# Convolution and attention layers on one Trainium2 core: the small maps written in two halves, the second tile's keys at a step's head, the first image's second chunk of values in a tile of its own

## The chip, the cores and the metric

One core of a Trainium2 chip runs the whole kernel as a single launch. The metric is device time in microseconds. The engines are named as the profile names them: PE multiplies matrices, DVE is the vector engine, ACT the scalar engine (it evaluates activations), POOL is GpSimd, and SP issues most of the DMA transfers. [...]

## The reference, cut to what matters

The input is 8 images of 256 channels and 64 x 64 pixels in float32. Two layers follow one another, each added to its input after a group normalisation.

```python
# layer 0: weights of a 3x3 window, made per pixel
x1, x2, x3 = conv1x1(x, w1, b1), conv1x1(x, w2, b2), conv1x1(x, w3, b3)   # 32, 32, 256 channels
h = relu(bn1(concat([x1, unfold3(reflect_pad(x2))])))                     # 320 channels
w = conv1x1(relu(bn2(conv1x1(h, cw1))), cw2, cb2)                         # 9 taps for 32 groups
out = einsum('bgskhw,bgkhw->bgshw', unfold3(zero_pad(x3)), w)
...
# layer 1: attention in a 7x7 window of each pixel, and a weighted depthwise branch
pe = einsum('dc,chw->dhw', Wp, position) + bp
q, k, v = conv1x1(x, Wq, bq) * 64 ** -0.5, conv1x1(x, Wk, bk), conv1x1(x, Wv, bv)   # 4 heads of 64
att = softmax(q . (unfold7(reflect_pad(k)) + unfold7(reflect_pad(pe))))
out_att = att . unfold7(reflect_pad(v))
wts = softmax over 9 of (Wfc x);  out_conv = sum over 9 of depthwise(relu(depthwise(x))) * wts
return rate1 * out_att + rate2 * out_conv
```

## The kernel before, in words

An image is cut into 8 bands of 8 rows (`NB`, `R`), 64 bands in all. The main loop runs over `g`, the band of layer 1; layer 0 runs 12 bands ahead of it (`AHEAD`), so that `g` begins at -12 and the last 12 bands have no layer 0 beside them. A band has 8 steps `s`: two halves of the channels (`ct`) times four pairs of 8 x 8 query tiles (`m`). I count steps from 0 and call them step 0 to step 7.

The order of the work is written out by hand. Within a step of layer 1 PE does, in even steps, the scores (L747, tile `sco`) and the weighted values (L796, into the PSUM bank `small`), and in every step two matrices of branch weights `pf` (L883) and the transposes of probabilities `ptp` (L784). ACT takes the exponentials of scores (L769) and of `pf` (L888), and scales the probabilities (L778). DVE masks the scores (L761), takes the reciprocal of their sum (L776) and does the taps of the depthwise branch (L840, L866).

`beside` puts the other work of a step into three lists. `head` is issued at the beginning of the step, before its exponentials; `mid` after the first `pf`; `end` behind everything. An entry may hand back a function that runs later, so that PE's part is issued first and the part of ACT or DVE behind it. `advance` divides a step into six places, and `after(n, f)` puts `f` off by n of them.

- `small_maps` (L324) makes, in step 0, two 1x1 convolutions of layer 0 for the band `g + 12` in the upper part of the bank `small`; PE's part is L332. `write_maps` (L339) copies them into the tile `x2` with eight activations on ACT (six at L347, two at L351): four for the upper four rows, four for the lower. Then POOL adds border columns and rows (L355, L356, L361, L362). `hidden_maps` (L411) reads `x2` for its relus (L422). The next use of `small` is L796 in step 2.
- `value_maps` makes the larger map of layer 0, in two parts: `p3` (L373) at the end of step 0 and in the middle of step 1, each copied to `x3n` by ACT (L378) and stored by SP (L380).
- `tap_weights` makes `pw` (L468) at the end of steps 1 to 5. DVE multiplies it with the map (L481, two products each) and POOL adds the products (L489).
- `queries` (L681, copied by ACT at L685) and `keys` (L703) are made once for each half of the channels. DVE finishes the keys with one large and three small operations (L711, L718). For the second half of the channels the keys stand in the middle of step 3, but in the first and last band of an image in step 2.
- `gn_affine` makes the coefficients of the group normalisations with small matmuls (L242) and DVE operations, in the fourth and the seventh band of an image, beginning in step 2.
- `values` (L598, copied by ACT at L605 into the tile `vc`) makes values for a band in two chunks. `store_values` stores them to DRAM with eight SP transfers (L618, L622), `mirror_rows` adds border rows there (L629), and `value_tile` loads them as `vt` (L640). For the first two bands of an image this is done during the last band of the image before, and for the first image in the band g = -1.
- `position` (L647) makes the position map `pe` on POOL (L655) for each of the first image's bands and stores it for the other images (L661, SP).

Most matmul results, `pf`, `ptp`, `p3`, `pw`, `pq`, `pk` and `pv`, share four PSUM buffers with the tag `gen`, which are handed out in turn: a tile waits for the readers of the fourth one before it. The bank `small` has one buffer, `vc` one, `ex` (SBUF, for the exponentials of `pf`) three.

Of the kernel before, what the change touches and what calls it, by code (L numbers as in the profile page):

```python
# [10 lines left out]
F32 = mybir.dt.float32  # L11
# [7 lines left out]
P = 128  # L19
C = 256  # L20
# [3 lines left out]
R = 8  # L24
BAND = R * W
NB = H // R
# [15 lines left out]
HR = R + 2  # L42
# [19 lines left out]
AHEAD = NB + 4  # L62
# [25 lines left out]
def conv_layers_kernel(ctx: ExitStack, tc: tile.TileContext, ins: dict, out: bass.AP):  # L88
    nc = tc.nc
# [130 lines left out]
    def after(n, f):  # L220
        later.append((place[0] + n, f))
# [102 lines left out]
    def small_maps(b, i, home):  # L324


        im = images[b]

        p12 = home[:, 2 * P :].rearrange("p (r c) -> p r c", r=R // 2)
        for kt in range(NCT):  # L330
            for u in range(2):
                nc.tensor.matmul(  # L332
                    p12[64 * u : 64 * u + 64], im.w12s[:, kt, :],
                    im.xc[i][:, kt, u * BAND // 2 : (u + 1) * BAND // 2],
                    start=(kt == 0), stop=(kt == NCT - 1),
                )
        return lambda: write_maps(b, i, p12)

    def write_maps(b, i, p12):  # L339
        im = images[b]  # L340
        t = im.x2[i] = w0.tile([P, HR, W], F32, tag="x2", name=f"x2_{b}_{i}", bufs=2)
        bias = im.bias
        for u in range(2):
            r, o = u * R // 2, 64 * u
            for q, (dst, src) in enumerate(((1, 0), (0, 0), (0, 1))):
                n = W - (q != 1)
                nc.scalar.activation(  # L347
                    t[32 * q : 32 * q + 32, r + 1 : r + 1 + R // 2, dst : dst + n],
                    p12[o : o + 32, :, src : src + n], AF.Identity, bias=bias[o : o + 32, 0:1],
                )  # L350
            nc.scalar.activation(  # L351
                t[96:128, r : r + R // 2, :], p12[o + 32 : o + 64], AF.Identity, bias=bias[o + 32 : o + 64, 0:1]
            )

        nc.gpsimd.tensor_copy(t[0:32, 1 : 1 + R, 0:1], t[0:32, 1 : 1 + R, 2:3])  # L355
        nc.gpsimd.tensor_copy(t[64:96, 1 : 1 + R, W - 1 : W], t[64:96, 1 : 1 + R, W - 3 : W - 2])  # L356

        if i == 0:
            nc.gpsimd.tensor_copy(t[0:96, 0, :], t[0:96, 2, :])
        else:  # L360
            nc.gpsimd.tensor_copy(t[0:96, 0, :], im.x2[i - 1][0:96, R, :])  # L361
            nc.gpsimd.tensor_copy(im.x2[i - 1][0:96, R + 1, :], t[0:96, 1, :])  # L362
        if i == NB - 1:
            nc.gpsimd.tensor_copy(t[0:96, R + 1, :], t[0:96, R - 1, :])
# [218 lines left out]
    def values(b, j, half):  # L583

        im = images[b]
        if half == 0:
            im.vc[j] = w1.tile([P, R // 2, C], F32, tag="vc", name=f"vc_{b}_{j}", bufs=1)
        vc, yp = im.vc[j], im.yp[min(j, NB - 1)]  # L590
        first, last, _ = value_rows(j)
        pv = ps.tile([P, 2, C], F32, tag="gen", name=f"pv_{b}_{j}_{half}", bufs=4)
        for g in range(2):
            r = first + 4 * half + 2 * g
            if r >= last:
                break
            for kt in range(NCT):
                nc.tensor.matmul(  # L598
                    pv[:, g], yp[:, kt, r : r + 2].rearrange("p r c -> p (r c)"), wv[:, kt],
                    start=(kt == 0), stop=(kt == NCT - 1),  # L600
                )
            n = g + 1

        def take():
            nc.scalar.copy(vc[:, 2 * half : 2 * half + n], pv[:, :n])  # L605

        return take
# [39 lines left out]
    def position(b, i):  # L647

        first, last = new_keys(i)
        n, a = last - first, i * R + first  # L650
        pe = images[b].pe[i] = w1.tile([P, KW - PAD, W], F32, tag="pe", name=f"pe_{b}_{i}", bufs=1)
        if b:
            nc.sync.dma_start(out=pe[:, :n], in_=kept[i])
            return
        nc.gpsimd.tensor_add(  # L655
            pe[:, :n],
            pecol.unsqueeze(1).to_broadcast([P, n, W]),
            perow[:, a : a + n].unsqueeze(2).to_broadcast([P, n, W]),
        )
        kept[i] = dram.tile([P, n, W], F32, tag=f"pe{i}", name=f"pe_{i}", bufs=1)  # L660
        nc.sync.dma_start(out=kept[i], in_=pe[:, :n])  # L661

    kept = {}

# [67 lines left out]
    half = [slice(0, HD), slice(HD, P)]  # L732
# [71 lines left out]
    def small_tile(nm):  # L804

        return ps.tile([P, 4 * P], F32, tag="small", name=f"small_{nm}")
# [117 lines left out]
    def beside(g, s):  # L924

        b, i = divmod(g, NB)
        bn, inx = divmod(g + 1, NB)
        head, mid, end = [], [], []

        early = i in (0, NB - 1)  # L930
        if g >= 0:
            if s == 2:
                mid.append(lambda: keys(b, i, 1) if early else queries(b, i, 1))
            if s == 3 and early:
                head.append(lambda: queries(b, i, 1))
            if s == 3 and not early:
                mid.append(lambda: keys(b, i, 1))
        edge = inx in (0, NB - 1)
        if 0 <= g + 1 < B * NB:
            if s == 5 - edge:  # L940
                mid.append(lambda: position(bn, inx))
            if s == 6:
                mid.append(lambda: keys(bn, inx, 0) if edge else queries(bn, inx, 0))
            if s == 7:
                head.append(lambda: queries(bn, inx, 0) if edge else keys(bn, inx, 0))

        made = [(b, i + 2, (4, 5))] if g >= 0 and i < NB - 1 else []
        if i == NB - 1 and 0 <= b + 1 < B:
            made = [(b + 1, 0, (3, 4)), (b + 1, 1, (5, 7))]
        for bb, j, d in made:  # L950
            if s in d and (j < NB or s == d[0]):
                mid.append(lambda bb=bb, j=j, d=d: values(bb, j, d.index(s)))
            if s == d[1]:
                end.append(lambda bb=bb, j=j: store_values(bb, j))
            if s == d[1] + 1 and j in (0, NB):
                end.append(lambda bb=bb, j=j: mirror_rows(bb, j))
            if s == 7 and j != 1:
                for u in range(NT // 2):
                    end.append(lambda bb=bb, j=j, u=u: value_tile(bb, j, u))
        if g >= 0 and i == 0 and s in (0, 2):  # L960
            for u in (s, s + 1):
                mid.append(lambda u=u: value_tile(b, 1, u))

        nxt = [(b, i + 2, 0)] if g >= 0 and i + 2 < NB else []
        if i == NB - 1 and 0 <= b + 1 < B:
            nxt = [(b + 1, 0, 0), (b + 1, 1, 2)]
        for bb, ii, d in nxt:
            if s == d:
                end.append(lambda bb=bb, ii=ii: load_rows(bb, ii))
            if s in (d + 1, d + 2):  # L970
                end.append(lambda bb=bb, ii=ii, d=d: normalise(bb, ii, s - d - 1))

        alone = g < 0
        if 0 <= g + AHEAD < B * NB:
            bq_, iq = divmod(g + AHEAD, NB)
            if alone and s == 0:
                mid.append(lambda: small_maps(bq_, iq, small_tile(f"{bq_}_{iq}"))())
            if s == (2 if alone else 0):
                (mid if alone else end).append(lambda: value_maps(bq_, iq, 0, alone))
            if s == (3 if alone else 1):  # L980
                mid.append(lambda: value_maps(bq_, iq, 1, alone))
        if 0 <= g + AHEAD - 1 < B * NB and s == (2 if alone else 1):
            bh, ih = divmod(g + AHEAD - 1, NB)

            def hidden():
                parts = hidden_maps(bh, ih, alone)
                if not alone:
                    convs.extend(parts)

            end.append(hidden)  # L990
        if 0 <= g + AHEAD - 2 < B * NB and s in TAPS_AT[g < -1]:
            u = TAPS_AT[g < -1].index(s)
            end.append(
                lambda: tap_weights(*divmod(g + AHEAD - 2, NB), u, g < -1, PRODUCTS_AT[g < -1][u])
            )
        return head, mid, end
# [24 lines left out]
    with tc.manual_schedule():  # L1021
# [17 lines left out]
        for n, f in enumerate(layer1_loads()):  # L1039
            after(4 * STEPS * (3 + n), f)  # L1040

        pending, before, conv, convs = [], None, None, []
        for g in range(-AHEAD, B * NB):
            b, i = divmod(g, NB)
            for s in range(STEPS):
                ct, m = divmod(s, NT // 2)
                head, mid, end = beside(g, s)
                steer(g, s)
                if g >= 0:
                    nm = f"{b}_{i}_{ct}_{m}"  # L1050
                    weighted = []
                    if m % 2 == 0:
# [3 lines left out]
                        small = small_tile(nm)  # L1056
                        weighted, pending = weigh_steps(pending, small), []
                        if s == 0 and g + AHEAD < B * NB:
                            mid.append(small_maps(*divmod(g + AHEAD, NB), small))
                        if s in (4, 6) and convs:  # L1060
                            convs.pop()(small)
                        if before is not None:
# [140 lines left out]
```

## Time and profile before

| | |
|---|---|
| median of 3 runs (lowest to highest) | 3902.41 us (3900.53 to 3902.47) |
| the profiled execution: its own time | 3901.4 us |
| its span, first to last instruction | 3899.5 us |
| mean granted clock of PE | 0.994 |
| first score matmul of the band g = 0 | 233.4 us |
| an ordinary band (2178.4 to 2236.0) | 57.6 us |

"Busy" is the time in which an engine had an instruction running. Ends of matmuls are modelled, so that the time between the starts of two matmuls is safer to read than the end of one. A line of the timeline has the start, the duration, the engine, the line in the kernel, the operation, the tile written and the tiles read, the size and the number of instructions in a row; in brackets stand the idle time before it and what ended it. A line of the waits has who waited for whom, the total in us, how often, and the longest.

### The profile page before, as it was taken

What the parts mean: (1) busy time and instruction counts of PE and PEld (TensorE: products, weight loads), DVE (VectorE), ACT (ScalarE), POOL (GpSimd) and SP (SyncE); (2) the same over time, 40 slices, a digit from 0 to 9 for tenths busy, and PEclk for the clock granted to TensorE, in tenths of its full rate; (3) what the DMA queues carried; (4) which work ended last, traced back from release to release, by engine and by line L of the source; (5) the groups of instructions that cost most, each with busy time, mean ns of one, the idle gap of its engine ahead of it and who ended that gap; (6) DMA issues with size and microseconds to landing.
All of it is one profiled execution on the core that took longest, in us unless ns stands there. A gap on an engine that the chain in (4) does not pass through costs nothing.

```text
span 3899.5 us, 71759 instructions
## 1 busy us (share of the span) xinstructions
PE 3774.0 (97%) x24620; PEld 2112.0 (54%) x24620; DVE 3415.8 (88%) x7125; ACT 2809.8 (72%) x6770; POOL 3118.1 (80%) x2100
## 2 busy tenths in 40 slices
PE   6889999999999999999999999999999999999998
PEld 3445555555555555555555555555555555555554
DVE  6879999889988989899998998989988889978777
ACT  4457777777777777777777777777777777677776
POOL 4768888888987988888888888978988888955665
PEclk9999999999999999999999999999999999999999
DMA  8754544544544543544544544454543543332221
GB/s 247 211 162 128 142 113 126 155 124 113 136 127 131 148 120 104 151 137 118 145 112 136 143 124 116 132 145 119 139 113 102 145 123 101 89 94 81 78 66 37
DMA packets 438926, 490.14 MB, mean 126 GB/s; under 512 B 62016, under 2 KB 324256, under 8 KB 438304
## 3 DMA queue, kind: packets, MB, share of 16 engines
q1 hardware_dynamic: 421984, 469.79, 43.4%
q10 hardware_dynamic: 16576, 15.76, 1.3%
q8 instruction: 194, 3.18, 0.3%
q14 instruction: 172, 1.41, 0.1%
HBM read 343.76 MB, written 145.10 MB: 125 GB/s over the span
## 4 chain that ended last, share of the span: by engine, by line
PE 38%; POOL 22%; DVE 20%; ACT 10%; issue 5%; DMA 4%; SPq 0%; ACTq 0%; POOLq 0%; DVEq 0%
PE pf L883 18%; POOL xg L489 10%; POOL ex L1099 7%; DVE prod L481 6%; DVE rec L904 4%; DVE acc L866 4%; PE small L796 3%; ACT x L347 3%; PE pv L598 3%; PE ptp L784 3%; PE sco L747 3%; PE pq L681 2%; PE pk L703 2%; DMA x<-x3n 2%; ACT ex L888 2%
## 5 line engine op out<-in xcount | busy, mean ns | idle before, releaser
L883 PE MATMUL pf<-yp,c_wfc 128*128 128x512 f32 x4096 | 1916.3, 594 | 16.7 <-ACT ex L888 10.3
L489 POOL TENSOR_TENSOR xg<-xg,prod 128x1024 f32<-128x1024 f32 x549 | 1201.0, 2188 | 108.7 <-DVE prod L481 82.7
L883 PEld LDWEIGHTS pf<-yp,c_wfc 128*128 128x128 f32 x4096 | 738.6, 190 | 715.7 <-issue 628.4
L1099 POOL TENSOR_TENSOR ex<-ex,ex 128x1024 f32<-128x1024 f32 x384 | 908.2, 2365 | 68.7 <-ACT ex L888 65.2
L840 DVE SCALAR_TENSOR_TENSOR acc<-yp,c_chan,acc 128x504 f32<-128x504 f32 (+3 forms) x1104 | 775.8, 703 | 63.3 <-ACT acc L831 42.9
L481 DVE SCALAR_TENSOR_TENSOR prod<-pw,c_par,x3q 128x1040 f32<-128x1040 f32 x576 | 737.3, 1287 | 92.3 <-PE pw L468 47.8
L866 DVE SCALAR_TENSOR_TENSOR acc<-hid,c_chan,acc 128x504 f32<-128x504 f32 (+3 forms) x1024 | 751.5, 734 | 18.1
L888 ACT ACTIVATE ex<-pf 128x512 f32<-128x512 f32 x1024 | 602.3, 588 | 220.7 <-PE pf L883 204.4
L769 ACT ACTIVATE prob<-prob,nmax 128x196 f32<-128x196 f32 x1024 | 459.2, 451 | 205.2 <-DVE nmax L761 204.9
L778 ACT ACTIVATE prob<-prob,tot 128x196 f32<-128x196 f32 x1024 | 413.0, 452 | 262.0 <-DVE tot L776 259.9
L905 POOL TENSOR_TENSOR tot<-tot,rec 128x256 f32<-128x256 f32 x254 | 185.7, 731 | 413.4 <-DVE rec L904 407.3
L904 DVE RECIPROCAL rec<-tot 128x256 f32<-128x256 f32 x256 | 445.8, 1741 | 8.2 <-POOL tot L899 6.6
L786 ACT COPY pt<-ptp 112x512 f32<-112x512 f32 x511 | 295.0, 577 | 111.3 <-PE ptp L784 110.8
L761 DVE CUSTOM_DVE_ANT_0 prob<-sco,c_mask 128x196 f32<-128x196 f32 x1024 | 324.8, 355 | 27.1 <-PE sco L747 27.0
L784 PEld LDWEIGHTS ptp<-ident,prob 128*112 128x112 f32 x2044 | 227.3, 133 | 184.8 <-issue 154.7
L784 PE MATMUL ptp<-ident,prob 128*112 128x128 f32 x2044 | 319.5, 279 | 0.2 <-ACT vc L605 0.2
L796 PEld LDWEIGHTS small<-pt,vt 112*64 112x64 f32 x8144 | 258.5, 138 | 83.5 <-issue 75.4
L796 PE MATMUL small<-pt,vt 112*64 112x64 f32 x8144 | 294.1, 225 | 7.2 <-DMA vt<-vd 7.2
L373 PE MATMUL p<-xc,w3s 128*128 128x512 f32 x512 | 248.1, 608 | 12.6 <-ACT ex L888 12.6
L598 PE MATMUL pv<-c_wv,yp 128*128 128x256 f32 x1056 | 252.3, 381 | 1.7 <-ACT yp L570 1.7
L899 POOL TENSOR_SCALAR tot<-tot 128x512 f32<-128x512 f32 x127 | 243.6, 1918 | 11.1
L468 PEld LDWEIGHTS pw<-h2n,c_c 128*128 128x128 f32 x1152 | 176.1, 192 | 138.2 <-issue 122.3
(136 smaller groups left out, 4655.4 us busy)
## 6 DMA issues: line engine op xcount, KB each, us to landing
vt<-vd SPq DMA_DIRECT2D x512, 112.0 KB
x3q<-x SPq DMA_DIRECT2D x128, 264.0 KB
xc<-in_x SPq DMA_DIRECT2D x64, 512.0 KB
xg<-in_xg SPq DMA_DIRECT2D x64, 512.0 KB
yp<-x SPq DMA_DIRECT2D x128, 256.0 KB
xr<-x SPq DMA_DIRECT2D x64, 512.0 KB
out_x<-xr SPq DMA_DIRECT2D x64, 512.0 KB
xs<-in_x SPq DMA_DIRECT2D x57, 512.0 KB
```

The costliest lines, as they stand in the source:

```text
L481: nc.vector.scalar_tensor_tensor(prod[:, :, :RUN], pw[:, j, :RUN].unsqueeze(1).to_broadcast([P, SHARE, RUN]), par[:, PCB2 + k : PCB2 + k + 1],
L489: nc.gpsimd.tensor_add(im.xg[i], im.xg[i], rows(prod))
L769: nc.scalar.activation(prob[:, h, :NKEY], prob[:, h, :NKEY], AF.Exp, bias=nmax[:, h : h + 1], scale=-1.0, accum_out=tot[:, h : h + 1],)
L778: nc.scalar.activation(prob[:, h, :NKEY], prob[:, h, :NKEY], AF.Copy, scale=tot[:, h : h + 1])
L784: nc.tensor.transpose(ptp[:, h, ch], prob[:, h, ch * CHUNK : (ch + 1) * CHUNK], ident)
L796: nc.tensor.matmul(po[half[h], :, t * TQ : (t + 1) * TQ], im.vt[i + ch, m][:n, t, (2 * ct + h) * HD : (2 * ct + h + 1) * HD], pt[:n, h, ch ...
L840: nc.vector.scalar_tensor_tensor(o, yp[:, ct, ra + dr : rb + dr, ca + dc : cb + dc], chan[:, ct, CW1 + k : CW1 + k + 1], o, ALU.mult, ALU.add,
L866: nc.vector.scalar_tensor_tensor(o, hid[:, ra + dr : rb + dr, ca + dc : cb + dc], chan[:, ct, CW2 + k : CW2 + k + 1], o, ALU.mult, ALU.add,)
L883: nc.tensor.matmul(pf, wfc[:, kt, 2 * m + j, ct * P : (ct + 1) * P], images[b].yp[i][:, kt, PAD : PAD + R], start=(kt == 0), stop=(kt == N ...
L888: nc.scalar.activation(ex[:, j].rearrange("p (r c) -> p r c", r=R), pf, AF.Exp)
L904: nc.vector.reciprocal(rec, v)
L1099: after(4, lambda ex=ex, exb=exb: nc.gpsimd.tensor_add(ex, ex, exb))
```

## The change

Five edits. The eight writes of the small maps are issued as two groups of four: the upper rows in step 0 as before, the lower rows with POOL's copies first in the middle of step 1. Outside layer 1 (g < 0) both groups stay together. The keys of the second half of the channels go from the middle to the head of step 3. For the first image, the second band's values get a buffer of `ex` in place of the single `vc`, and their second chunk and its stores come in step 6 in place of step 7. The store of the position map is issued nine places later.

```diff
-        return lambda: write_maps(b, i, p12)
-
-    def write_maps(b, i, p12):
-        im = images[b]
-        t = im.x2[i] = w0.tile([P, HR, W], F32, tag="x2", name=f"x2_{b}_{i}", bufs=2)
-        bias = im.bias
-        for u in range(2):
+        im.x2[i] = w0.tile([P, HR, W], F32, tag="x2", name=f"x2_{b}_{i}", bufs=2)
+        return lambda u: write_maps(b, i, p12, u)
+
+    def write_maps(b, i, p12, half):
+        im = images[b]
+        t, bias = im.x2[i], im.bias
+        for u in half:
...
+        if half[-1] == 0:
+            return
...
         if half == 0:
-            im.vc[j] = w1.tile([P, R // 2, C], F32, tag="vc", name=f"vc_{b}_{j}", bufs=1)
+            tag, bufs = ("ex", 3) if (b, j) == (0, 1) else ("vc", 1)
+            im.vc[j] = w1.tile([P, R // 2, C], F32, tag=tag, name=f"vc_{b}_{j}", bufs=bufs)
...
-        nc.sync.dma_start(out=kept[i], in_=pe[:, :n])
+        after(9, lambda: nc.sync.dma_start(out=kept[i], in_=pe[:, :n]))
...
             if s == 3 and not early:
-                mid.append(lambda: keys(b, i, 1))
+                head.append(lambda: keys(b, i, 1))
...
-            made = [(b + 1, 0, (3, 4)), (b + 1, 1, (5, 7))]
+            made = [(b + 1, 0, (3, 4)), (b + 1, 1, (5, 7 if g >= 0 else 6))]
...
-                mid.append(lambda: small_maps(bq_, iq, small_tile(f"{bq_}_{iq}"))())
+                mid.append(lambda: small_maps(bq_, iq, small_tile(f"{bq_}_{iq}"))((0, 1)))
...
-        pending, before, conv, convs = [], None, None, []
+        pending, before, conv, convs, maps = [], None, None, [], []
...
                 head, mid, end = beside(g, s)
+                if s == 1:
+                    mid, maps = maps + mid, []
...
-                            mid.append(small_maps(*divmod(g + AHEAD, NB), small))
+                            write = small_maps(*divmod(g + AHEAD, NB), small)
+                            mid.append(lambda write=write: write((0,)))
+                            maps.append(lambda write=write: write((1,)))
```

## The prediction, made before the changed kernel was run

> **What bounds the kernel now.** I read the busy shares first, then the waits of the tensor engine alone, then the order of time in one ordinary band. On the page, and in the waits of PE from 233 us to the end (total us, times, longest):
>
> ```profile
> PE 3774.0 (97%) x24620; PEld 2112.0 (54%) x24620; DVE 3415.8 (88%) x7125; ACT 2809.8 (72%) x6770; POOL 3118.1 (80%) x2100
> ```
>
> ```profile
> PE p L373 <- ACT ex L888: 12.6, 52, 0.9
> ...
> PE small L796 <- DMA vt<-vd: 7.2, 2, 6.7
> ...
> PE sco L747 <- DVE kb L718: 5.2, 29, 0.2
> PE pg_b L242 <- ACT ex L888: 2.3, 6, 0.4
> ```
>
> PE is the bound: 64 bands run after 233 us, and an ordinary band (2178.4 to 2236.0) takes 57.6 us of which PE is busy 57.25. Only time that PE waits can be won. Three of these waits belong to work that the change moves. They are larger than listed, because ends of matmuls are modelled, so I measure them from start to start. The first one, at 2178.4 + 8 us (start, us, operation):
>
> ```profile
> 2184.85 1.39 ACT L347 ACTIVATE x<-small,bias 32x252 f32<-32x252 f32 x3
> ...
> 2188.18 0.47 ACT L351 ACTIVATE x<-small,bias 32x256 f32<-32x256 f32 x1
> ...
> 2188.54 0.60 PE L784 MATMUL ptp<-ident,prob 128*112 128x128 f32 x4
> ...
> 2188.67 0.60 ACT L888 ACTIVATE ex<-pf 128x512 f32<-128x512 f32 x1
> ...
> 2189.32 1.98 PE L373 MATMUL p<-xc,w3s 128*128 128x512 f32 x4 [0.18 <-ACT ex L888]
> ...
> 2191.14 1.88 PE L883 MATMUL pf<-yp,c_wfc 128*128 128x512 f32 x4
> ```
>
> The eight small-map writes hold ACT from 2184.85 to 2188.65. The exponential of step 0's second `pf`, whose matmuls ended by 2185.3, waits behind them. Four PSUM buffers `gen` go round, and the second `p3` of the band (step 1) needs the one that this exponential empties: it starts at 2189.32, 0.05 us after it. The transposes before it take 0.78 us from start to start, where the same four take 0.44 before L703 (2203.14 to 2203.58); the four L373 then take 1.82, where the pair in step 0 took 1.72 (2185.11 to 2186.83). So 0.34 + 0.10 = **0.44 us a band**.
>
> **What the Trainium skill says.** Perfetto Trace Analysis, section Identifying Performance Opportunities (its Optimization Strategy part): a gap that repeats on the engine that should be saturated can mean too few buffers for the next tile; the 52 waits of L373 are such a gap. The same page, Optimizing Scalar/DVE Operations: where ACT isn't saturated but makes bubbles elsewhere, splitting its work can let something finish sooner; ACT is 72% busy here. PSUM — Partial Sum Buffer, Engine vs sequencer instructions: the ACT, DVE and POOL queues are strict FIFO; the trace agrees, since the ready exponential stood behind eight writes. DMA: Bandwidth & Descriptors, Latency and other measured facts: a DMA has about 2 us of fixed cost; no landing time is listed here, but PE resumes at 255.78, 3.0 us after the first value-tile load was issued at 252.75.
>
> **Part 1, the halves.** Nothing is added or removed: the eight activations stay (0.46 us each), the POOL copies behind them too (0.19 to 0.23 each). Four of the eight, 1.9 us, leave step 0 and go into the middle of step 1. Walking ACT's queue on with the trace's durations: the `pf` exponential runs 2186.7 to 2187.3; PE wants the buffer at 2188.98 (0.44 after 2188.54). The wait is gone with 1.6 us to spare. Worth 0.44 in 45 bands; 0.70 in six first bands of an image (transposes at 2128.78, L373 at 2129.81: 1.03 instead of 0.44, and the 0.10); about 1.2 in the very first (0.95 idle there), which I count under part 3. 19.8 + 4.2 = **24.0 us**.
>
> What queues behind the moved writes in step 1: ACT comes there early with the change (its probabilities end at about 2190.7), writes until 2192.6, then goes on with `x3n` to 2193.3 and the exponential of step 1's second `pf` to 2193.9, 0.2 later than the 2193.66 of now. Its buffer is wanted by L681 in step 2, which starts at 2197.5 now: 3 us of slack. The `small` bank is wanted by L796 of step 2, 2194.26 now, 2193.8 then: **1.2 us of slack**, the tightest. The POOL copies end by 2193.0, in the 5.3 us that POOL now waits for L904; they are needed by the relus L422, at 2195.8. The SP store of the first `x3n` comes sooner. DVE idles 2.74 us in step 1 waiting for ACT's exponentials; they come 1.9 us sooner, so DVE gets ahead by about 0.7 us, where it is stopped by L815 waiting for PE. That lead helps L681 of an image's first bands, which waits 0.4 us for DVE's keys: 6 x 0.3 = **1.8 us**.
>
> **Part 2, the keys.** Four matmuls (1.72 us) and four DVE operations (0.73 + 0.53, from L711 and L718) move to the head of step 3, in 48 bands. Now they end last:
>
> ```profile
> 2207.12 0.53 DVE L718 SCALAR_TENSOR_TENSOR kb<-pk,c_chan,pe 128x16 f32<-128x16 f32 x3
> ...
> 2207.80 0.92 PE L747 MATMUL sco<-kb,qb 64*64 64x196 f32 x16 [0.17 <-DVE kb L718]
> ```
>
> L468 to L747 is 0.79 where it is 0.54 elsewhere (2192.86 to 2193.40): 0.25 lost. At the head they follow the second product (ends 2205.06 now, about 2204.4 then), end at about 2205.6, and scores want them at 2207.1: 27 ordinary bands x 0.25 and two late ones x 0.3, **7.3 us**. The price: two tap pairs and the reciprocal L776 fall behind them, so the probabilities come at about 2207 and the last exponential 0.5 us later than now; step 4's transposes want them at 2209.6. Hidden.
>
> In 12 bands (the fourth and the seventh of six images) a normalisation matmul L242 stands between. It waits now for the second product, although the wait is put down to ACT:
>
> ```profile
> 2320.30 1.29 DVE L481 SCALAR_TENSOR_TENSOR prod<-pw,c_par,x3q 128x1040 f32<-128x1040 f32 x1
> ...
> 2321.67 0.38 PE L242 MATMUL pg_a<-d_a,c_gmat 128*128 128x2 f32 x2 [0.83 <-ACT ex L888]
> ```
>
> With the keys at the head the buffer rotation changes: the `pf` after L242 takes the buffer of `pk`, which DVE's keys empty 1.2 us after that product. With the 0.7 us lead this puts `pf` at 2322.15, against 2321.91 now: these bands lose their 0.44 and 0.07 more, 12 x 0.51 = **-6.1 us**. Bounds: +6 (the lead is larger) to -11 (no lead).
>
> **Part 3, the start.** SP's queue and its waits there:
>
> ```profile
> SPq L661 <- POOL pe L655: 16.0, 1, 16.0
> ```
>
> ```profile
> 224.64 0.32 SPq L661 DMA_DIRECT2D pe<-pe x1
> 225.06 1.32 SPq L618 DMA_DIRECT2D vd<-vc x2
> ...
> 240.86 5.62 SPq L640 DMA_DIRECT2D vt<-vd x8
> 246.59 1.33 SPq L618 DMA_DIRECT2D vd<-vc x2
> 247.97 4.07 SPq L622 DMA_DIRECT2D vd<-vc x6
> 252.75 3.12 SPq L640 DMA_DIRECT2D vt<-vd x4
> ```
>
> SP stands 16 us on one store until POOL has made the position map, with the first value stores behind it (ready when ACT's copy ends, 220.7). ACT stands 8.99 us until they have freed the single `vc`. The second tile's stores go out after eight tile loads, its loads last, and PE waits 6.67 + 0.48 us. After: the position store sits nine slots on; the first stores go at 220.8; the other tile needs no buffer freed; its stores (5.4 us of issue) stand ahead of the eight loads. From the issue times the two loads that PE needs go out at about 245 to 247 and land, at 3 us, by 250; PE, starting about 1 us sooner (ACT's wait held L685), arrives at 246.7. So 255.78 becomes about 249: **6.8 us**, the 1.2 of the first band within it. Bounds: 0 (another load is as late) to 10.5. The delayed position stores of the other seven bands, and a buffer of `ex` held until its stores have read it (about 237, wanted at 249), cost nothing.
>
> Sum: 24.0 + 1.8 + 7.3 - 6.1 + 6.8 = 33.8, say **34 us**. The profiled run took 3901.4 around a span of 3899.5; span 3865.5, run 3867.4. The median shown is 1.0 above that run: **3868 us**.
>
> **Rivals.** (a) As worked out, 3852 to 3882. PE's steadiness speaks for it: bands of one kind repeat to 0.1 us. 0.60. (b) Part 1 is given back: ACT or DVE ends a wait in step 2 or 3 by some 0.3 us, and keys win nothing: 24 - 16 + 7 = 15 us, 3887. For it: DVE has no gap from 2190.9 to 2211. Against: the slacks above. 0.23. (c) Slower: the second half is still in the `small` bank when L796 of step 2 comes, and PE stops there. It decides from 1.2 us of lateness on; each further microsecond costs 52 us, so it turns the sign at 1.2 + 0.65. The probabilities stand ahead of the writes and wait for DVE's reciprocal; DVE busy there by 2 us more would do it. 2.2 us late gives +52 - 34 = +18, 3920. Against: DVE is idle 2.74 us just there. 0.08. (d) The change doesn't do what it says: L373's buffer turns out to wait for something else that is as late, and only the keys' and the start's part of (b) comes: 3900. The 0.05 us between exponential and matmul, 52 times, speaks against it: 0.09.
>
> **Numbers.** About 0.2% is what a measurement of this kernel can tell from no change, so faster means under 3894.6. (a) and (b) give 0.83; within 0.2% 0.08, most of (d); slower 0.09, (c) and what is left of (d). The range of 8 in 10 goes from 3852 (all bounds good) to 3887, taking in the likeliest (b).
>
> **What would show it.** Right: L373 no longer waits for L888; L347 in two groups a step apart; no wait of L747 for L718; ordinary bands at 56.9 instead of 57.6; L242's bands no shorter than now; SP's 16 us and ACT's 8.99 us gone, and PE's wait for `vt` under 3 us (`vt` loads behind the second tile's stores, not before them). Wrong: new waits of L796 for ACT in step 2, or of L883 for DVE's keys in ordinary bands.

## The result and the profile after

| | before | changed |
|---|---|---|
| median, first comparison | 3901.8 us (4 runs) | 3857.84 us (3855.78 to 3860.75, 4 runs) |
| ratio, 95% interval | | 0.9888, 0.9871 to 0.9905 |
| median, second comparison | 3900.05 us (9 runs) | 3859.9 us (3856.07 to 3862.81, 4 runs) |
| ratio, 95% interval | | 0.9897, 0.9882 to 0.9911 |
| profiled execution: own time and span | 3901.4, 3899.5 us | 3855.78, 3854.0 us |

The change is faster by 44.0 us in one comparison and 40.2 in the other; forecast were 34 us and 3868. The total is near, but not because every term was right. The largest miss, the bands with L242, came out 10.4 us better than forecast; two others, the first bands' L681 and the start, came out 1.8 and 1.9 us worse, so that the errors cancel in part. And the keys' 7 us came, but from another edit than forecast.

Lines have moved by two or three in the changed kernel: L747 is now L750, L883 L886, L888 L891, L373 L375, L796 L799, L718 L721. First come the busy times on its page, then the longest waits of PE from 227 us to the end (total, times, longest; three rows of 0.8 us and less are not shown):

```profile
PE 3754.7 (97%) x24620; PEld 2108.4 (55%) x24620; DVE 3432.5 (89%) x7125; ACT 2814.5 (73%) x6770; POOL 3118.1 (81%) x2100
```

```profile
PE pf L886 <- ACT ex L891: 10.7, 16, 0.7
PE pf L886 <- DVE prod L483: 6.3, 6, 1.1
PE pw L470 <- ACT ex L891: 2.8, 1, 2.8
PE pg_a L242 <- ACT ex L891: 2.6, 6, 0.6
PE pg_b L242 <- ACT ex L891: 1.9, 6, 0.3
PE pq L684 <- ACT ex L891: 1.4, 6, 0.2
PE small L799 <- DMA vt<-vd: 0.9, 1, 0.9
```

The 52 waits of `p3` and the 29 of the scores for `kb` are no longer there. By an ordinary band I mean one that has layer 0 beside it, is neither the first nor the last of an image and has no normalisation; there are 27. Fourth and seventh bands below are those with a normalisation, six of each. The one from 2146.0 to 2202.9 takes 56.9 us where it took 57.6, as forecast, and PE is recorded busy for all of it. Its steps 0 and 1 in the timeline:

```profile
2152.46 1.40 ACT L347 ACTIVATE x<-small,bias 32x252 f32<-32x252 f32 x3
...
2153.87 0.47 ACT L351 ACTIVATE x<-small,bias 32x256 f32<-32x256 f32 x1
...
2154.36 0.60 ACT L891 ACTIVATE ex<-pf 128x512 f32<-128x512 f32 x1
...
2156.16 0.60 PE L787 MATMUL ptp<-ident,prob 128*112 128x128 f32 x4
...
2156.58 0.17 DVE L779 RECIPROCAL tot<-tot 128x2 f32<-128x2 f32 x1 [0.81 <-ACT prob L772]
2156.59 1.88 PE L375 MATMUL p<-xc,w3s 128*128 128x512 f32 x4
...
2158.23 1.43 ACT L347 ACTIVATE x<-small,bias 32x252 f32<-32x252 f32 x3
```

Four writes hold ACT until 2154.34, the exponential of step 0's second `pf` follows at once, and `p3` starts at 2156.59, 0.43 us after the transposes and 1.6 us after the buffer is free. This is what the prediction had worked out. The line of DVE shows something more: it waits 0.81 us for ACT's score exponentials where it waited 2.74 in the same place of the kernel before:

```profile
2190.89 0.17 DVE L776 RECIPROCAL tot<-tot 128x2 f32<-128x2 f32 x1 [2.74 <-ACT prob L769]
```

**Where the 45.5 us between the two profiled spans are.** I compare from the first score matmul of a band to that of the next. A second trace of the changed kernel shows how far to trust this: bands after the first repeat within 0.04 us. The 63 bands after the first give 36.4 us. By the median, ordinary bands are 0.71 shorter, an image's first band 0.67, its fourth 0.98, its seventh 0.61 and its eighth 0.46; the last twelve, without layer 0, are unchanged. The first band and what lies ahead of it from the small maps of the band g = -1 (L332) give 5.4. The remaining 3.75 us lie ahead of that, where the order of work has not changed: that L332 came at 200.18 in this trace and at 205.30 in the second one. I take them for scatter and not for an effect.

### The profile page after: what moved, and what is told of

Read it like the earlier page. It is cut to its first block, busy times and chain, and to the rows that moved or that the text cites. A ratio compares the mean times of both kernels' runs of the same rounds, so it can differ in the third digit from the quotient of the medians.

```text
span 3854.0 us, 71730 instructions
## 1 busy us (share of the span) xinstructions
PE 3754.7 (97%) x24620; PEld 2108.4 (55%) x24620; DVE 3432.5 (89%) x7125; ACT 2814.5 (73%) x6770; POOL 3118.1 (81%) x2100
## 4 chain that ended last, share of the span: by engine, by line
PE 76%; POOL 8%; DVE 8%; ACT 3%; issue 2%; DMA 2%; SPq 1%; ACTq 0%; POOLq 0%; DVEq 0%
PE pf L886 37%; PE small L799 6%; PE ptp L787 5%; PE sco L750 5%; POOL xg L491 5%; PE pq L684 4%; PE p L375 4%; PE pk L706 4%; PE pv L601 4%; DVE prod L483 3%; PE pw L470 2%; POOL ex L1106 2%; PE small L332 1%; DVE acc L869 1%; PE small L434 1%
## 5 line engine op out<-in xcount | busy, mean ns | idle before, releaser
L886 PE MATMUL pf<-yp,c_wfc 128*128 128x512 f32 x4096 | 1917.7, 594 | 17.0 <-ACT ex L891 10.7
L886 PEld LDWEIGHTS pf<-yp,c_wfc 128*128 128x128 f32 x4096 | 739.9, 190 | 717.5 <-issue 655.2
L891 ACT ACTIVATE ex<-pf 128x512 f32<-128x512 f32 x1024 | 603.3, 589 | 249.7 <-PE pf L886 232.3
L799 PEld LDWEIGHTS small<-pt,vt 112*64 112x64 f32 x8144 | 258.6, 138 | 78.0 <-issue 60.5
L799 PE MATMUL small<-pt,vt 112*64 112x64 f32 x8144 | 294.2, 225 | 1.3 <-DMA vt<-vd 0.9
L470 PEld LDWEIGHTS pw<-h2n,c_c 128*128 128x128 f32 x1152 | 175.2, 191 | 140.7 <-issue 123.7
L357 POOL COPY x<-x 32x8 f32<-32x8 f32 x64 | 12.1, 189 | 288.3 <-ACT x L347 288.3
```

Of the source, the lines that this page charges most:

```text
L799: nc.tensor.matmul(po[half[h], :, t * TQ : (t + 1) * TQ], im.vt[i + ch, m][:n, t, (2 * ct + h) * HD : (2 * ct + h + 1) * HD], pt[:n, h, ch ...
L886: nc.tensor.matmul(pf, wfc[:, kt, 2 * m + j, ct * P : (ct + 1) * P], images[b].yp[i][:, kt, PAD : PAD + R], start=(kt == 0), stop=(kt == N ...
L891: nc.scalar.activation(ex[:, j].rearrange("p (r c) -> p r c", r=R), pf, AF.Exp)
```

## The experiments

**The halves alone** (the kernel before; `write_maps` split, nothing else).

> Before, with the eight small-map writes in two groups a step apart and nothing else changed. My sum for this part (24.0 + 1.8, and 1.2 in the very first band): 27 us, so about 3875; L375 has no wait, an ordinary band takes 57.6 - 0.44 = 57.16, the first bands of images 0.70 less, the fourth and seventh bands 0.44 less or a little more (0.44 + 0.3 if what L242 waits for comes sooner with DVE's or ACT's lead). Rival, part 1 is given back (a wait of step 2 or 3 ends by ACT or DVE a little later): ordinary bands 57.4 or more, 8 us in all, 3894. Rival, the buffer waits for something else: 0.

Measured: 3867.02 us, ratio 0.9907 (0.9890 to 0.9923). From band 1 on 37.8 us are gained, more than by the whole change. Ordinary bands are 0.71 shorter, not 0.44, because 27 of the 29 waits of the scores for `kb` go too, with the keys still in the middle of step 3. The other two, in the last twelve bands, stay:

```profile
PE sco L749 <- DVE kb L720: 0.5, 2, 0.2
```

The fourth and the seventh bands are 0.90 shorter. First bands of an image gain 0.68, which is the 0.70 of `p3` alone: L683 still waits 0.40. The very first band gained nothing where 1.2 us was expected: from L332 of the band g = -1 to the first score of the second band it took 99.5 us in this one trace, and 97.7 before.

**The keys alone.**

```diff
             if s == 3 and not early:
-                mid.append(lambda: keys(b, i, 1))
+                head.append(lambda: keys(b, i, 1))
```

> Before, with the second tile's keys at the head of step 3 and nothing else changed. Theory of the prediction: ordinary bands 57.6 - 0.25 = 57.35 (27 x 0.25 = 6.8 us gained), but in the fourth and seventh bands the pf behind L242 waits for the keys, 0.9 us longer than now (no lead of DVE here), 12 x 0.9 = 11 us lost: 4 us slower, 3906. Rival, from the trace after the change (pf starts there before the keys have ended, and L242 starts right behind the exponential of step 3's first pf): L242 waits for that exponential alone and the keys' place is nothing to it; the fourth and seventh bands change by less than 0.2, and the whole is about 7 us faster, 3895.

Measured: 3902.51 us, ratio 0.9999 (0.9990 to 1.0007). Both expectations failed on the ordinary bands: none changes by more than 0.07 us, and the mean by 0.02. The fourth and seventh bands are 0.07 and 0.08 shorter, the eighth 0.08 longer; so L242 does not wait for the keys, as the rival had it. The scores' wait is gone, but the 0.25 us are lost again 12 us later in the band. ACT's waits for POOL from 300 us to 3850, first before, then with the keys moved, and then the place in an ordinary band (it starts at 2181.64):

```profile
ACT ex L888 <- POOL ex L1099: 11.5, 42, 0.8
```

```profile
ACT ex L888 <- POOL ex L1099: 18.5, 40, 0.8
```

```profile
2220.43 2.37 POOL L1099 TENSOR_TENSOR ex<-ex,ex 128x1024 f32<-128x1024 f32 x1
...
2222.83 0.60 ACT L888 ACTIVATE ex<-pf 128x512 f32<-128x512 f32 x1 [0.55 <-POOL ex L1099]
...
2223.48 1.98 PE L883 MATMUL pf<-yp,c_wfc 128*128 128x512 f32 x4
```

PE's second `pf` of step 5 wants the PSUM buffer that ACT's exponential empties; that exponential wants the SBUF buffer `ex` that POOL's sum frees. POOL comes to this sum at the end of a row of work with hardly a gap since step 2 (the row begins 16.96 us into the band, before as with the keys moved), so bringing PE forward does not bring POOL forward. ACT waits 7.0 us more for POOL (18.5 against 11.5), about the 6.8 that I had counted as a gain.

**The same with less work on POOL**, and its control, the kernel before with less work on POOL. Both leave out one addition in `dynamic_sum`, 1.27 us of POOL twice a band, and with it the depthwise branch of the output:

```diff
             engine.tensor_mul(oc, oc, tot)
-            engine.tensor_add(xr[:, ct], xr[:, ct], oc)
```

> The kernel before, with POOL's last addition of a half band (L910, 1.27 us, twice a band) left out, so that the depthwise branch is missing from the output. Theory: before the change the scores of step 4 wait for DVE's keys (L718), which POOL doesn't hold up; ordinary bands stay at 57.6 within 0.1 and the wait of L747 stays. It is the control for the next run. Rival, POOL already costs PE time there: ordinary bands 57.4 or less.

> Before, with the second tile's keys at the head of step 3, and the same addition left out. With the keys moved alone, the wait of the scores went and as much came back in step 5, where the trace has PE's second pf behind ACT's exponential, and that behind POOL's sum of two ex buffers (L1099), the last of a row of POOL work without a gap since step 2. Theory: POOL's row took the 0.25 us back; with 1.27 us less in it the exponential doesn't wait, and ordinary bands fall from 57.6 to 57.35, 27 x 0.25 = 7 us against the control. Rival, ACT or DVE's own order sets the second pf of step 5: no difference to the control.

Measured: the control took 3886.96 us, with the keys at the head 3878.73. Against the control, ordinary bands are shorter by 0.22 to 0.26, and all bands after the first together by 7.3 us. This settles it: the keys' place is worth 0.25 us a band where POOL has room, and nothing where it has not. The control showed more than I expected. Its ordinary bands are all but unchanged (0.06 shorter at most, and 0.33 in one of the first image), but the eighth bands are 1.2 us shorter: six waits of PE for DVE's product, 6.4 us in the kernel before, are gone there. Before that product DVE had waited for POOL (0.51 us in the band that starts at 2057.42), so POOL was setting PE's time in that place. The very last band is 4.8 us shorter too, but it is measured to the end of the span and its last addition is on DVE, so it says nothing about POOL.

**The start in two parts**: the position map's store nine places later alone, and the second tile of values (own buffer, one step sooner) alone.

> Before, with the store of the position map nine places later and nothing else changed. The first value stores go out at about 221 in place of 225, so the single vc comes free about 4 us sooner and ACT's wait of 8.99 shrinks to about 5: the first score matmul comes 2 to 4 us before 233.5; the second tile's stores still stand behind eight tile loads, so PE still waits 5 us or more for vt: in all 4 us faster (0 to 6). Rival, SP's 16 us lie beside other work and the buffer or the order of the loads sets the end: 0.

> Before, with the first image's second chunk of values a step sooner and its tile in a buffer of ex, and nothing else changed. ACT's 8.99 us wait for the single vc goes (first score matmul up to 6 us before 233.5), the second tile's stores stand ahead of the eight loads, but all of them still start behind the 16 us of SP, at 225: PE's wait for vt falls from 7 to about 3. In all 6 us faster (4 to 9); together with the position store alone it should add up to the 9.1 us of the change. Rival, the values alone do nothing while SP stands: less than 2.

Measured: 3900.63 and 3900.3 us; ratios 0.9996 (0.9987 to 1.0004) and 0.9995 (0.9986 to 1.0003), neither of which can be told from none. The traces tell more if the scatter ahead is left out, by measuring from L332 of the band g = -1 to the first score of the second band. The five kernels with the old start take 97.2 to 99.5, mean 98.05; six with the new start (all but the one with moved statistics) 92.3 to 93.6, mean 93.1. So the whole start is worth about **4.9 us**. This is not cleanly part 3: all six of the second group have the halves as well, and of the first group only the run with the halves alone, which is its longest, 99.5. Without that run the difference is 4.6. The store alone takes 94.1 (4.0 less than the mean), the values alone 96.1 (1.9 less). Each of these two is one trace, and the five with the old start differ by 2.3. My expectation that the first scores come several us sooner was wrong: from that L332 they come after 28.8 to 29.5 with the old start, 26.9 to 29.6 with the new one. The gain lies in the first band, where PE no longer waits for `vt`. In the changed kernel SP's wait, and its queue:

```profile
SPq L621 <- ACT vc L608: 8.0, 1, 8.0
```

```profile
217.02 1.31 SPq L621 DMA_DIRECT2D vd<-vc  x2
218.37 3.23 SPq L625 DMA_DIRECT2D vd<-vc  x6
226.10 0.54 SPq L664 DMA_DIRECT2D pe<-pe  x1
228.56 1.66 SPq L621 DMA_DIRECT2D vd<-vc  x2
230.56 3.72 SPq L625 DMA_DIRECT2D vd<-vc  x6
237.56 8.40 SPq L643 DMA_DIRECT2D vt<-vd  x12
```

The order is the forecast one: both tiles' stores ahead of all twelve loads. PE's wait for `vt` falls from 7.2 us to 0.9, but a new one of 2.8 stands in the same band (L470, in the list above), so that less comes out than was worked out. (In the trace with the values in step 6, below, the two are 1.7 and 1.8.)

**All eight writes in step 1** (the changed kernel):

```diff
-                            mid.append(lambda write=write: write((0,)))
-                            maps.append(lambda write=write: write((1,)))
+                            maps.append(lambda write=write: write((0, 1)))
```

> The changed kernel, with all eight small-map writes in step 1 and none in step 0. Theory (rival (c) of the prediction is a real limit): in the trace after the change the fourth late write ends 1.3 us before L799 of step 2, and ACT is tied to PE ahead of the writes, so four more writes of 0.47 end about 1.9 us later and PE waits about 0.6 us in L799 for ACT L351, 52 times: 31 us slower than the changed kernel, about 3889; L375 still has no wait. Rival, the slack is much larger (ACT gains what it no longer writes in step 0, and the eight start sooner): within 5 us of the changed kernel, no wait of L799.

Measured: 3920.94 us, ratio to before 1.0051 (1.0036 to 1.0066), 63 us slower than the changed kernel. PE's waits after 310 us, and an ordinary band (it starts at 2190.46):

```profile
PE small L799 <- ACT x L351: 23.2, 51, 0.7
PE pf L886 <- DVE prod L483: 19.9, 33, 0.7
```

```profile
2206.40 1.15 PE L799 MATMUL small<-pt,vt 112*64 112x64 f32 x32 [0.45 <-ACT x L351]
...
2211.91 0.17 DVE L779 RECIPROCAL tot<-tot 128x2 f32<-128x2 f32 x1 [1.05 <-ACT prob L772]
...
2216.77 1.30 DVE L483 SCALAR_TENSOR_TENSOR prod<-pw,c_par,x3q 128x1040 f32<-128x1040 f32 x1
...
2218.22 1.96 PE L886 MATMUL pf<-yp,c_wfc 128*128 128x512 f32 x4 [0.62 <-DVE prod L483]
```

The limit of rival (c) is real and lies where it was reckoned: start to start L799 loses 0.52 us (0.6 expected). But an ordinary band loses 1.37 in all, and the whole 63 us where 31 were expected. ACT goes on about 1.7 us late, DVE waits for its score exponentials, DVE's second product of step 3 ends late, and PE's `pf` stops for 0.78 more until that product has ended. So ACT's lateness reaches PE twice, once directly and once through DVE.

**The normalisation's matmuls two places later** (the changed kernel, `after(3, a1)` made `after(5, a1)` in `gn_affine`; `a3` follows it).

> The changed kernel, with both L242 matmuls of a normalisation two places later, behind the second pf of step 2 and behind the pw of step 3. In the built order the second pf of step 3 then takes the buffer that the exponential of step 3's first pf empties, where L242 took it before. Theory (that exponential ends the wait, whoever asks for its buffer): L242 no longer waits, but L886 stands in its place, 0.4 to 0.6 us, 12 times, so the fourth band gains nothing (within 0.15). In the seventh band the rotation of step 5 changes too: the pf that waited 0.87 us behind L548 takes an older buffer, 6 x 0.87 = 5 us faster in all. Rival (the wait belongs to L242's own place, or to DVE's product): the 0.55 go as well, 12 us faster.

Measured: 3862.54 us, ratio to before 0.9902 (0.9888 to 0.9917), by its bands after the first 3.4 us slower than the changed kernel. The first two rows of PE's waits after 310 us:

```profile
PE pf L886 <- ACT ex L891: 9.2, 21, 0.7
PE pgc L548 <- DVE tot L779: 7.1, 6, 1.2
```

The first part came nearly as expected: L242 waits no more, the `pf` in its place waits 0.47 where L242 waited 0.55, and the fourth bands are only 0.19 shorter. The second did not: the `pf` behind L548 no longer waits, but L548 itself does, 1.35 us in place of that 0.87, for DVE, which comes to its input later, and seventh bands are 0.41 longer. Two of the six seventh bands are 1.94 longer, which makes up 3.1 of the 3.4 us; the cause of that is open, and in the combination below, with the same edit, it does not appear.

**The next image's first values in step 6 of the last band**, then that with two other edits: the normalisation's matmuls two places later, as above, and the statistics of the band g = -1 taken later.

```diff
-            made = [(b + 1, 0, (3, 4)), (b + 1, 1, (5, 7 if g >= 0 else 6))]
+            made = [(b + 1, 0, (3, 4)), (b + 1, 1, (6, 7) if g >= 0 else (5, 6))]
```

> The changed kernel, with the first chunk of the next image's second tile of values in step 6 in place of step 5 of an image's last band (step 5 and 6 kept for the first image). In the changed kernel the first pf of step 6 takes the buffer of step 5's pw, whose last reader is DVE's second product in step 6: 1.25 us, 7 times. Here it takes an older one. Theory: that wait goes and the eighth bands are 1.2 us shorter, 7 x 1.2 = 8 us faster. Rival: the next pf of step 6 takes the buffer of the first and waits for its exponential instead, so that less than 3 us is left.

> The changed kernel with three edits: the normalisation's L242 behind step 2's and step 3's last matmuls, the second tile's first values in step 6 as above, and the statistics L287 of the band g = -1 taken fifteen places after their load in place of nine (DVE waits 5.3 us for that load, and PE 2.8 us in the very first band for what DVE does behind it). If each does what I expect of it, 5 + 8 + 2.5 = 15 us faster than the changed kernel, 3843; if the waits only change their place, 0 to 5.

Measured: 3851.32 us (0.9875, 0.9860 to 0.9890) and 3853.07 us (0.9879, 0.9862 to 0.9895). The eighth bands are 1.31 shorter and no other band after the first moves by more than 0.04: 8 us, as expected. The combination gives nothing beyond that. With the statistics moved, the first band's wait of 2.8 us in L470 is gone and PE waits 3.8 for `vt` in its stead; the normalisation costs what it did alone.

**The version that comes out of this**: the changed kernel with the keys back in the middle of step 3 and the values in step 6; and the changed kernel again beside it.

> The changed kernel with the keys back in the middle of step 3 and the next image's first values in step 6 of the last band. By the bands of the runs with the halves alone and with the values in step 6: the seventh bands 0.30 shorter (6 x 0.3 = 1.8), the fourth 0.07 longer (6 x 0.07 = 0.4), the eighth 1.3 shorter (7 x 1.3 = 9.1): 10.5 us faster than the changed kernel, about 3847. If the keys' place matters after all once the rotation of buffers changes, ordinary bands 0.1 to 0.25 longer and only 3 to 6 us are left.

> The changed kernel once more, for the comparison on one chip, and for the start: the first scores came at 227 us in its first trace, but at 231 to 236 in four kernels with the same start. If that is scatter of the loads, the bands repeat within 0.05 us and the first scores come at 230 to 236; if the change itself brought them forward by 6 us, at 227 to 228 again.

Measured: 3851.34 us, ratio to before 0.9874 (0.9859 to 0.9888), against 3859.9 (0.9897) for the changed kernel on the same chip: 8.6 us faster, where the bands after the first sum to 9.4. The seventh bands are 0.29 shorter, the fourth 0.08 longer, the eighth 1.31 shorter, ordinary ones unchanged. The first three rows of PE's waits after 310 us; none for DVE's product is left:

```profile
PE pf L886 <- ACT ex L891: 9.7, 15, 0.7
PE pg_a L242 <- ACT ex L891: 2.5, 6, 0.6
PE pq L684 <- ACT ex L891: 1.4, 6, 0.2
```

## Why the prediction was right or wrong

| term | forecast | measured |
|---|---|---|
| wait of `p3` (L373), 45 + 6 bands | 24.0 | all gone; about 24: 0.46 in eighth bands and 0.67 in first ones, where nothing else is won |
| L681 of first bands | 1.8 | 0: still 0.40 each |
| keys' wait, 27 ordinary bands and two of the last twelve | 7.3, from part 2 | about 7, from part 1; nothing in those two |
| L242, 12 bands | -6.1 | +4.3: 6 x (0.98 - 0.44) + 6 x (0.61 - 0.44) |
| start | 6.8 | 4.9, what the halves do to the first band within it |
| sum | 33.8 | about 40; by bands and start 36.4 + 4.9 = 41.3 |

**Right: part 1's own wait.** The exponential behind the eight writes was the whole of L373's stall, and ordinary bands came to 56.9. The Trainium skill (Perfetto Trace Analysis, Optimizing Scalar/DVE Operations) speaks of breaking up instructions on an ACT that is not saturated and makes bubbles elsewhere. Here no instruction was broken up: eight were issued in two groups of four. The run with the halves alone shows that this served the same end, at the same ACT load (2813.7 us busy, 2809.8 before).

**Failed: whose gain the keys' 0.25 is.** The step said that at the head of step 3 the keys end 1.5 us before the scores, so that 0.25 is won. The keys moved alone won nothing, since POOL, and behind it ACT, give PE the next buffer no sooner. The halves alone won it with the keys unmoved. That this term appears in the sum with its forecast size is therefore luck. The prediction did see that DVE gets ahead by about 0.7 us with the halves (L779 of step 1 is 1.9 us sooner within the band, the products of step 3 by 0.73), but spent this only on two other waits. POOL follows DVE: its row begins 16.06 us into the band in place of 16.96. With both forward, keys and POOL's sum are each in time wherever the keys stand. A hint of it was in the profile: 42 waits of ACT for POOL's sum, an engine that the prediction looked at only for an idle stretch. It is no more than a hint, for the changed kernel has 42 such waits too (11.2 us), and PE loses nothing by them in ordinary bands. In (b), "keys win nothing" was right for part 2 by itself; the gain that it took away was there all the same.

**Failed: L242.** There were two errors. The first: the profile put the wait down to ACT's exponential, and I overrode this with DVE's second product, which ended at nearly the same time (2321.59 against 2321.62, L242 at 2321.67). In the fourth bands the two end within 0.02 us of each other in every kernel where L242 waits there, because both follow the same DVE operation, the row maxima `nmax`; so these bands cannot tell them apart. A seventh band of the changed kernel can:

```profile
2458.21 1.30 DVE L483 SCALAR_TENSOR_TENSOR prod<-pw,c_par,x3q 128x1040 f32<-128x1040 f32 x1
...
2459.30 0.60 ACT L891 ACTIVATE ex<-pf 128x512 f32<-128x512 f32 x1 [0.26 <-PE pf L886]
...
2459.95 0.38 PE L242 MATMUL pg_b<-d_b,c_gq 128*128 128x1 f32 x2 [0.31 <-ACT ex L891]
```

L242 starts 0.05 us after the exponential has ended and 0.44 after the product has, and so it is in all six seventh bands. It waits for the exponential of step 3's first `pf`.

The second error: I took the four `gen` buffers for a strict ring. In a ring, L242 would take the buffer of the fourth tile before it, `pw`, which the product reads. What it waits for shows that it takes that of the first `pf`, which is nearer. The run with the normalisation moved confirms this: the second `pf` of step 3, which then stands behind the same four tiles, also starts 0.05 us after that exponential, and in the seventh bands 0.44 after the product. So the sentence in the description of the kernel before, that a tile waits for the fourth one before it, is too simple. Nor does the `pf` behind L242 wait for the keys, as I had it; in a fourth band of the changed kernel it starts while they are still being written:

```profile
2286.95 0.38 PE L242 MATMUL pg_a<-d_a,c_gmat 128*128 128x2 f32 x2 [0.39 <-ACT ex L891]
...
2287.19 1.96 PE L886 MATMUL pf<-yp,c_wfc 128*128 128x512 f32 x4
...
2287.45 0.52 DVE L721 SCALAR_TENSOR_TENSOR kb<-pk,c_chan,pe 128x16 f32<-128x16 f32 x3
```

In the fourth bands L242 comes 0.9 us sooner within the band (27.23 in place of 28.12): the exponential stands in ACT's order behind the score exponentials, and these wait for `nmax`, so that DVE's lead reaches PE in full. I had expected these bands to gain nothing.

What the keys' move does cost is 0.3 us in each seventh band (0.61 gained in place of 0.91). With the keys moved ahead of it, the first `pf` of step 3 comes 1.7 us later, and in the lines above ACT waits 0.26 for it before the exponential. In the last version, with the keys back in the middle, the exponential follows the score exponentials without a wait, and the 0.3 us are won back. Against 0.08 won in each fourth band, part 2 costs the changed kernel about 1.3 us in all.

**Failed, small: L681.** Its 0.40 stayed. It is the same fault: I gave the wait to DVE's keys, where the profile said ACT's exponential. That exponential reads step 2's second `pf` and cannot begin before PE has made it, so a lead of DVE does nothing for it. In the two bands of the last twelve, with the keys at the head, 0.3 each was expected and nothing came.

**Start: right order, too large.** The loads come where they were put, but 6.8 us were forecast and about 4.9 came, because PE arrives at another wait of the same band.

**The rivals.** (c) did not happen, and its place and slack were right: in the changed kernel's ordinary band the late writes end at 2160.15 and L799 starts at 2161.43, 1.3 us later. Its price was too low: 0.52 us of lateness cost 1.37 a band, not 0.52. (d) did not happen either; its figure was a slip, since the start's 7 us alone lead to 3895 and not to 3900.

## What to carry to other kernels

Do an edit alone, on chip, before crediting it with a wait that it seems to remove: here the wait vanished with another edit, and what the move alone won was lost again, in full, to an engine that PE does not wait for directly. When PE waits for ACT, ask what ACT waited for; a row of work without gaps on an engine at 80% can set the time of a part of the loop, although the average leaves room. And where two events end within 0.1 us of each other ahead of a wait, look for a place in the same trace where they end apart before overriding the releaser that the profile names.

## What the runs showed of the hardware

The stretch ahead of the first band scatters far more than the bands. In the twelve traces in which the order of work is the same up to there, all but the two with the normalisation moved, L332 of the band g = -1 came at 200.2 to 207.3 us, while the bands after the first repeat to 0.04 between two traces of one kernel. Single profiled spans can differ by 7 us for that reason alone. The Trainium skill (Perfetto Trace Analysis, GPSIMD Engine Instruction) calls the recorded span of a GpSimd instruction unreliable and advises timing from start to start. In the place that this case rests on, the record does fit: POOL's sum at 2220.43 lasts 2.37, and the exponential that waits for it starts at 2222.83, 0.03 us after its end. From the end of the ACT exponential to the start of the matmul that waits for it there are 0.05 us in every such wait of L242, in the kernel before as in the changed one.
